# Scores, softmax and weighted values of an attention layer staggered by one step, and the experts' biases summed on another engine

## The chip, the cores and the metric

The kernel runs on one core of one Trainium2 chip. A core has five engines that work side by side and wait for each other by semaphores: TensorE (PE; its weight loads are a row of their own, PEld), VectorE (DVE), ScalarE (ACT), GpSimd (POOL) and SyncE (SP), which here only issues DMAs. The metric is the device time of one execution in microseconds (us).

## The reference, cut to what matters

Two layers work on 8 x 1024 tokens of 256 numbers, in float32. The first is a per-token attention over channels with a layer norm. The second is a transformer block: attention over the 8 positions of the first axis (1024 independent columns, 4 heads of 64), a layer norm, and a mixture of 8 experts with a capacity of 1024 tokens each, then two more layer norms. The parts that the change touches:

```python
qkv = x @ w.T + b
scores = jnp.einsum('nhld,nhmd->nhlm', q, k) / np.float32(np.sqrt(HD))
attn = jax.nn.softmax(scores, axis=-1)
o = jnp.einsum('nhlm,nhmd->nhld', attn, v).transpose(2, 0, 1, 3).reshape(L, N, D)
...
h = jnp.einsum('ecd,edf->ecf', disp, w1) + b1[:, None, :]
y = (jnp.einsum('ecf,efd->ecd', h, w2) + b2[:, None, :]).reshape(E * cap, D)
```

There is no nonlinearity between w1 and w2. So an expert is one matrix w1 w2 (256 x 256) and one bias row b1 w2 + b2, and the kernel works both out once, ahead of the tokens.

## The kernel before, in words

Three phases follow each other. `phase_a` (up to 4336 us) is the first layer. `phase_b` (to 4951 us) is the second layer's attention, its first norm, the router's logits, and, mixed in, the experts' products. `phase_c` routes the tokens, applies the experts and the last norms. The change is in `phase_b` and in a few lines of `phase_c`.

In `phase_b` the order of the instructions on every engine is the order of the program (`manual_schedule`). The loop runs over j from -1 to 8. A group j is 128 columns of the 1024, with 8 positions each: 1024 tokens. Iteration j does the attention of group j, prepares group j + 1 (`nxt`: `turn_x`, `project_qk`, `project_v`), finishes group j - 1 (`prv`: `output`, `normal`, `turn_y`, `logits`) and works out expert j. It has four steps n: a pair of heads c and a half ib of the group's blocks. A step's attention is:

- `scores` (L620): ten products into the tile `sc` (two banks of PSUM), the largest of each row negated by VectorE (L645, L646)
- `weights` (L651), twice: four exponentials each on ScalarE (L654), with their sums
- `normed` (L662): VectorE divides by the sums (L664, L665)
- `turn_s` (L667): eight transposes by TensorE into `pt` (two banks), copied by ScalarE to `sT` (L673)
- `weighted` (L676): sixteen products with the values, copied by ScalarE into `oT` (L691)

Between these the function `some(k)` takes the next k entries from the step's list, which `fills(j)` (L794) writes out by hand. What remains of the list follows at the step's end. All entries and `weighted` use PSUM tiles `fill`, of which there are two. [...] `sc` 2, `pt` 2, `pw` 1, `pb` 1, `fill` 2.

`expert(e, piece)` (L764) adds two of the eight blocks of w1 w2 to `pw` (L773) and, with two products, their part of all biases to `pb` (8 x 256, L781). The left side of those is `b1z`, a block of b1 in one column of eight and zero in the others. `load_expert` (L756) brings a piece's w1 and w2 in at the start of each step, on SP's queue, behind a piece of zeros for `disp_d` (L862, in two of the four steps). In the same queue stand the stores of y (L727). In `phase_c`, sixteen small products (L1000) and four copies (L1007) spread the bias rows `b12` over all partitions; the experts' results get them at L1061.

`output` (L703) begins with `residual`: POOL adds the output bias to x (L698). VectorE then adds the product (L716) and takes statistics (L66, L68), and POOL makes the reciprocal root (L70, L72). `normal` (L719) scales on VectorE (L724), applies gain and bias on POOL (L726) and stores y. `turn_y` (L729) needs that y.

Of the kernel before, what the change touches and what calls it, by code (L numbers as in the profile page):

```python
# [21 lines left out]
FP = mybir.dt.float32  # L22
# [4 lines left out]
ALU = mybir.AluOpType  # L27
# [3 lines left out]
P = 128  # L31
# [13 lines left out]
@with_exitstack  # L45
def fused_kernel(ctx: ExitStack, tc: tile.TileContext, a: dict, out: bass.AP):
    nc = tc.nc

    const = ctx.enter_context(tc.tile_pool(name="const", bufs=1))
    small = ctx.enter_context(tc.tile_pool(name="small", bufs=4))  # L50

    ident = const.tile([P, P], FP, name="ident")
    make_identity(nc, ident)
    mhalf = const.tile([P, 1], FP, name="mhalf")
    nc.gpsimd.memset(mhalf, -0.5)

    dram = ctx.enter_context(tc.tile_pool(name="dram", bufs=1, space=bass.MemoryType.DRAM))
    x1_d = dram.tile([L * N, D], FP, name="x1_d")
    y1_d = dram.tile([L * N, D], FP, name="y1_d")
    disp_d = dram.tile([2 * E * CAP, D], FP, name="disp_d")  # L60
    moe_d = dram.tile([E * CAP + 1, D], FP, name="moe_d")

    def norm_scalars(r):

        st = small.tile([P, 6], FP, name="st")
        nc.vector.bn_stats(out=st, in_=r)  # L66
        mv = small.tile([P, 2], FP, name="mv")
        nc.vector.bn_aggr(out=mv, in_=st)  # L68
        ve = small.tile([P, 1], FP, name="ve")
        nc.gpsimd.tensor_scalar(ve, mv[:, 1:2], EPS, None, ALU.add)  # L70
        rs = small.tile([P, 1], FP, name="rs")
        nc.gpsimd.tensor_tensor(rs, ve, mhalf, ALU.pow)  # L72
        return mv[:, 0:1], rs

    phase_a(tc, a, ident, x1_d, norm_scalars)

    late = ctx.enter_context(tc.tile_pool(name="late", bufs=1))
    w12 = late.tile([P, DC, E, D], FP, name="w12")
    b12 = late.tile([E, D], FP, name="b12")
    lg = late.tile([P, NT, E], FP, name="lg")  # L80
    phase_b(tc, a, ident, x1_d, y1_d, disp_d, w12, b12, lg, norm_scalars)
    phase_c(tc, a, ident, x1_d, y1_d, disp_d, moe_d, w12, b12, lg, norm_scalars, out)


def phase_a(tc, a, ident, x1_d, norm_scalars):
# [417 lines left out]
        store(NT - 1)  # L503


def phase_b(tc, a, ident, x1_d, y1_d, disp_d, w12, b12, lg, norm_scalars):

# [7 lines left out]
    with (  # L515
        tc.tile_pool(name="bw", bufs=1) as wp,
        tc.tile_pool(name="bgroup", bufs=2) as gp,
        tc.tile_pool(name="bx", bufs=3) as xp,
        tc.tile_pool(name="bwork", bufs=2) as kp,
        tc.tile_pool(name="bps", bufs=1, space=PSUM) as p1,  # L520
        tc.tile_pool(name="bfill", bufs=2, space=PSUM) as pf,
        tc.manual_schedule(),
    ):
        wi = wp.tile([P, DC, 3 * D], FP, name="wi")
# [9 lines left out]
        nc.sync.dma_start(wout, a["out_wT"].rearrange("(c p) f -> p c f", p=P))  # L534
        wg = wp.tile([P, DC, E], FP, name="wg")
        nc.sync.dma_start(wg, a["wg"].rearrange("(c p) e -> p c e", p=P))
        nc.sync.dma_start(b12, a["b2"])

        b1r = wp.tile([P, FC, E], FP, name="b1r")
        nc.sync.dma_start(b1r, a["b1T"].rearrange("(c p) e -> p c e", p=P))  # L540
        b1z = wp.tile([P, FC, E, E], FP, name="b1z")
        nc.gpsimd.memset(b1z, 0.0)
        nc.gpsimd.tensor_copy(b1z.rearrange("p c e f -> p c (e f)")[:, :, 0 : E * E : E + 1], b1r)


        rep = wp.tile([P, L, B], BF, name="rep")
# [3 lines left out]
        for h in range(2):  # L550
            r = slice(h * HW, h * HW + B)
            nc.vector.tensor_copy(rep[r], ident[r, None, r].to_broadcast([B, L, B]))
            nc.vector.tensor_scalar(other[r], rep[r], -1.0, MASKED, ALU.add, ALU.mult)
        pb = p1.tile([E, D], FP, name="pb")
        zeros = wp.tile([P, 1024], FP, name="zeros")
        nc.gpsimd.memset(zeros, 0.0)

# [8 lines left out]
        def turn_x(j, l0):  # L566
            if l0 == 0:
                G["xT", j] = wp.tile([P, DC, NB, L, B], FP, name="xT")
                G["qk", j] = gp.tile([P, DC, 2, N], FP, name="qk")
                G["v", j] = gp.tile([P, NB, D], FP, name="v")  # L570
            ps = pf.tile([P, 512], FP, name="fill")
            for l in range(2):
                for c in range(DC):
                    n = 2 * l + c
                    nc.tensor.transpose(
                        ps[:, n * P : (n + 1) * P], G["x", j][:, l0 + l, c * P : (c + 1) * P], ident
                    )
            for l in range(2):
                nc.vector.tensor_copy(
                    G["xT", j][:, :, :, l0 + l, :],  # L580
                    ps[:, l * D : (l + 1) * D].rearrange("p (c b n) -> p c b n", c=DC, n=B),
                )
# [17 lines left out]

        def project_v(j, b0):
            xT = G["xT", j].rearrange("p c b l n -> p c b (l n)")
            ps = pf.tile([P, 512], FP, name="fill")
# [15 lines left out]

        def scores(j, c, ib):  # L620
            qk = G["qk", j]
            sc = p1.tile([P, 2, 512], FP, name="sc")
            prs = [slice(h * HW, (h + 1) * HW) for h in range(2)]
            for h in range(2):
                nc.tensor.matmul(
# [39 lines left out]
            nc.vector.tensor_tensor(s, s, sm[:, :, None].to_broadcast([P, 8, P]), ALU.mult)  # L665

        def turn_s(state):  # L667
            s = state[2]
            pt = p1.tile([P, 2, 512], FP, name="pt")
            for g in range(8):  # L670
                nc.tensor.transpose(pt[:, g // 4, (g % 4) * P : (g % 4 + 1) * P], s[:, g, :], ident)
            sT = kp.tile([P, 8, P], FP, name="sT")
            nc.scalar.copy(sT, pt)  # L673
            return sT
# [89 lines left out]
        def expert(e, piece):  # L764
# [5 lines left out]
            for i in range(2):  # L770
                fc = piece * 2 + i
                for d in range(DC):
# [8 lines left out]
                nc.tensor.matmul(  # L781
                    pb,
                    b1z[:, fc, e, :],
                    w2[:, i, :],
                    start=e == 0 and fc == 0,
                    stop=e == E - 1 and fc == FC - 1,
                    skip_group_check=True,
                )
            if piece == 3:
                nc.scalar.copy(w12[:, :, e, :], pw.rearrange("p (c d) -> p c d", c=DC))  # L790
                if e == E - 1:
                    nc.vector.tensor_tensor(b12, pb, b12, ALU.add)

        def fills(j):  # L794

# [7 lines left out]
            def put(part, ok, fn, *args):  # L803
                if ok:
                    o[part].append((fn, *args))

            put(0, O, output, prv, 0)
            put(0, N, turn_x, nxt, 0)
            put(0, N, turn_x, nxt, 2)
            put(0, O, output, prv, 2)  # L810
            put(0, O, normal, prv, 0)
            put(0, N, turn_x, nxt, 4)
            put(0, N, turn_x, nxt, 6)
            put(0, X, expert, j, 0)
# [27 lines left out]
            put(3, N, project_qk, nxt, 1, 1, 1)  # L842
            return o

        for j in range(-1, NJ + 1):
            if j < 0:
                load_x(0)
# [2 lines left out]
            for n in range(4):  # L850
                work = list(parts[n])

                def some(k):
                    for _ in range(k):
                        if work:
                            fn, *args = work.pop(0)
                            fn(*args)

                if 0 <= j < NJ:
# [7 lines left out]
                    st = scores(j, c, ib)  # L867
                    some(1)
                    weights(st, 0)
                    some(1)  # L870
                    weights(st, 1)
                    normed(st)
                    some(3)
                    sT = turn_s(st)
                    some(1)
                    weighted(j, c, ib, sT)
                some(len(work))
                if n == 2 and 0 <= j and j + 2 < NJ:
                    load_x(j + 2)


def phase_c(tc, a, ident, x1_d, y1_d, disp_d, moe_d, w12, b12, lg, norm_scalars, out):


    nc = tc.nc
# [2 lines left out]
    with (  # L888
# [103 lines left out]
                tc.declare_no_dep(one.ins, other.ins, reason="rows of their own")  # L992
            scattered.append(one)


        bias = op.tile([P, E, D], FP, name="bias")
        for e in range(0, E, 2):
            ps = pp.tile([P, 512], FP, name="ps")
            for i in range(2):
                nc.tensor.matmul(  # L1000
                    ps[:, i * D : (i + 1) * D],
                    ident[0:E, e + i : e + i + 1].to_broadcast([E, P]),
                    b12,
                    start=True,
                    stop=True,
                )
            nc.vector.tensor_copy(bias[:, e : e + 2, :], ps.rearrange("p (e d) -> p e d", e=2))  # L1007
        disp_v = disp_d.rearrange("(e s p) d -> e p s d", p=P, s=SH)
        moe_v = moe_d[0 : E * CAP, :].rearrange("(e s p) d -> e p s d", p=P, s=SH)
        NH = E * ST // SH  # L1010
# [223 lines left out]
```

## Time and profile before

| | us |
|---|---|
| median of 3 runs | 5320.8 (5317.32 to 5326.3) |
| profiled execution, its own time | 5320.41 |
| its span | 5318.7 |
| TensorE busy | 5016.6 (94%) |
| VectorE / ScalarE / POOL busy | 2975.2 / 3361.0 / 3367.1 |
| second phase, first scores to end of the last `weighted` | 4374.8 to 4914.7 |

The span is the time from the first to the last instruction of the profiled execution; 1.7 us of that execution lie around it. "PE fill L683 <- ACT sT L673" means that TensorE stood still before it wrote `fill` at line 683, until ScalarE's write of `sT` at line 673 was done; the numbers after it are the total in us, how often, and the longest. A row of the timeline has the start and the length in us, the engine, line, operation, what is written and read, the shape and how many instructions are merged. A bracket at its end tells the idle time before it and who ended that. A matmul's length holds its way through the pipeline, so the distance between starts tells what a stream of them costs.

### The profile page before, as it was taken

The page shows a single profiled execution, that of the slowest core. Times are in us where ns is not written, and L with a number is a line of the kernel's source. Part 1 is how long each engine was busy: PE and PEld are TensorE (multiplying, and loading weights), DVE is VectorE, ACT ScalarE, POOL GpSimd, SP SyncE. Part 2 cuts the span into 40 slices and gives each one's busy share as a digit, 9 for nine tenths or more (in the row PEclk, how much of TensorE's full clock was granted, in tenths as well). Part 3 has the DMA queues.
Part 4 walks back from the last instruction along what each step waited for, and adds up shares of the span by engine and source line. Part 5 has one row for each costly group of instructions (what it writes and reads, how often), then busy time and mean ns, then how long its engine had stood idle before and what let it go on. Part 6 is the DMA issues. An engine that isn't in the chain of part 4 may idle for free. (4 is left out here: it accounts for less than half of the span.)

```text
span 5318.7 us, 190637 instructions
## 1 busy us (share of the span) xinstructions
PE 5016.6 (94%) x80212; PEld 3384.1 (64%) x80212; DVE 2975.2 (56%) x5849; ACT 3361.0 (63%) x4106; POOL 3367.1 (63%) x6939
## 2 busy tenths in 40 slices
PE   8999999999999999999999999999999978898177
PEld 4666666666666666666666666666666645565166
DVE  5666666666666666666666666666666633433145
ACT  4777777777777777777777777777777743333025
POOL 5776766677777767677676777667676632333625
PEclk9999999999999999999999999999999989999589
DMA  2222222222222222222222222222222221221463
GB/s 74 47 48 48 48 48 48 48 48 48 48 48 48 48 47 48 48 48 48 48 49 47 49 48 48 48 47 49 48 48 48 47 77 65 70 80 56 136 219 98
DMA packets 603424, 313.55 MB, mean 59 GB/s; under 512 B 388154, under 2 KB 562371, under 8 KB 602563
## 3 DMA queue, kind: packets, MB, share of 16 engines
q1 hardware_dynamic: 396130, 147.14, 12.1%
q0 software_dynamic: 202752, 151.40, 9.6%
q8 instruction: 627, 10.27, 0.8%
q10 hardware_dynamic: 3680, 2.83, 0.2%
q14 instruction: 235, 1.92, 0.1%
HBM read 82.76 MB, written 50.33 MB: 25 GB/s over the span
## 5 line engine op out<-in xcount | busy, mean ns | idle before, releaser
L324 ACT ACTIVATE e<-pair 128x1024 f32<-128x1024 f32 x3072 | 2977.4, 1021 | 1237.4 <-PE pair L308 1237.4
L368 POOL DMA_DIRECT2D nd<-S x4096 | 1953.0, 484 | 612.1 <-DVE S L358 420.0
L308 PE MATMUL pair<-R,L 32*128 32x128 f32 (+1 forms) x32768 | 1607.0, 323 | 1.8 <-POOL event L279 1.8
L358 DVE COPY S<-sum 128x512 f32<-128x512 f32 x1024 | 707.1, 691 | 1467.4 <-PE sum L347 1131.6
L308 PEld LDWEIGHTS pair<-R,L 32*128 32x128 f32 x32768 | 1272.4, 186 | 47.9 <-POOL event L279 2.3
L338 PE MATMUL sum<-e,V 128*32 128x256 f32 x16384 | 1285.7, 385 | 4.9 <-DVE S L358 4.9
L265 POOL DMA_DIRECT2D R<-qm x2048 | 973.9, 483 | 73.8 <-issue 38.7
L347 PE MATMUL sum<-e,V 128*32 128x128 f32 x16384 | 823.6, 273 | 0.0
L347 PEld LDWEIGHTS sum<-e,V 128*32 128x32 f32 x16384 | 533.0, 110 | 352.8 <-issue 1.8
L338 PEld LDWEIGHTS sum<-e,V 128*32 128x32 f32 x16384 | 406.5, 109 | 236.8 <-DVE vT L206 41.8
L296 PE MATMUL pair<-late,sel 32*128 32x256 bf16 (+1 forms) x6144 | 499.3, 313 | 9.6 <-ACT e L324 9.6
L219 DVE COPY V<-vT 32x128 f32<-32x128 f32 x2048 | 457.1, 223 | 28.1
L377 DVE RECIPROCAL att<-nd 128x256 f32<-128x256 f32 x256 | 447.4, 1748 | 7.2 <-DMA nd<-S 3.3
L296 PEld LDWEIGHTS <-sel 32*128 32x128 bf16 x6144 | 155.4, 91 | 460.4 <-issue 445.0
L279 POOL MEMSET event<- 1x1 f32 x256 | 22.8, 89 | 615.3 <-DMA R<-qm 403.1
L188 PE MATMUL ps<-wk,xT 128*128 128x512 f32 x512 | 257.8, 626 | 11.7 <-DMA wk<-in_Wk 10.9
L199 PEld LDWEIGHTS ps<-xT,wv 128*128 128x128 f32 x2048 | 238.2, 191 | 44.4 <-issue 41.8
L199 PE MATMUL ps<-xT,wv 128*128 128x128 f32 x2048 | 262.6, 281 | 1.6 <-DVE qm L232 0.8
L70 POOL TENSOR_SCALAR ve<-mv 128x1 f32<-128x1 f32 x128 | 39.4, 308 | 354.6 <-DVE mv L68 353.2
L231 PE MATMUL ps<-wq,xT 128*128 128x512 f32 x512 | 255.7, 622 | 5.8 <-DVE k L189 5.8
L408 PE MATMUL ps<-wo,attT 128*128 128x256 f32 x1024 | 256.7, 394 | 0.7 <-ACT attT L391 0.7
L408 PEld LDWEIGHTS ps<-wo,attT 128*128 128x128 f32 x1024 | 185.3, 191 | 63.3 <-issue 41.8
(171 smaller groups left out, 3962.4 us busy)
## 6 DMA issues: line engine op xcount, KB each, us to landing
R<-qm POOLq DMA_DIRECT2D x2048, 32.0 KB
nd<-S POOLq DMA_DIRECT2D x4096, 16.0 KB
L<-k SPq DMA_DIRECT2D x4088, 8.0 KB
xT<-in_xT SPq DMA_DIRECT2D x64, 128.0 KB
xr<-in_x SPq DMA_DIRECT2D x64, 128.0 KB
x_d<-x1o SPq DMA_DIRECT2D x64, 128.0 KB
x<-x_d SPq DMA_DIRECT2D x8, 1024.0 KB
disp_d<-zeros SPq DMA_DIRECT2D x16, 512.0 KB
```

The source lines that it names most:

```text
L199: nc.tensor.matmul(ps[:, i * P : (i + 1) * P], w["v"][:, c, ch * P : (ch + 1) * P], xT_of[t][:, c, :], start=c == 0, stop=c == DC - 1,)
L219: nc.vector.tensor_copy(V[32 * aa : 32 * aa + 32, qd % 2, :, qd // 2, :, aa, 0:4], src[32 * qd : 32 * qd + 32, :, ww, :, aa, :],)
L265: moved.append((None, nc.gpsimd.dma_start(R[:, b, s, b, :], q[:, b, s, cols])))
L296: nc.tensor.matmul(bank[u].rearrange("p (n i) -> p n i", i=n)[:, :, 0:32], sel[pr].rearrange("p a j -> p (a j)"), late[pr, None, :].to_bro ...
L308: one = nc.tensor.matmul(bank[u][:, x * 4 * n : (x + 1) * 4 * n].rearrange("p (b i) -> p b i", i=n), Lt[pr, 2 * (h0 + h) + jb].rearrange(" ...
L324: nc.scalar.activation(e, pair[i], AF.Exp)
L338: nc.tensor.matmul(dst[32 * u : 32 * u + 32], Vs[ww][:, 0, h0 + h, u, :], e0[u // 2][:, u % 2, x * 256 : (x + 1) * 256].rearrange("p (b i) ...
L347: nc.tensor.matmul(dst[32 * u : 32 * u + 32, :, 32:], Vs[ww][:, 1, h0 + h, u, :], e1[u // 2][:, u % 2, h * 128 : (h + 1) * 128].rearrange( ...
L358: nc.vector.tensor_copy(S[:, :, 2 * which : 2 * which + 2, :].rearrange("p b h i -> p h b i"), ps.rearrange("p (h b i) -> p h b i", h=2, b=4),
L368: nc.gpsimd.dma_start(tok[:, b, s, h0 * C1 : (h0 + G) * C1], Sx[:, 4 if s else b, b, :])
L377: nc.vector.reciprocal(att[:, cols], nd[:, 1, cols])
L408: nc.tensor.matmul(ps[:, :D], attT[:, c, :], wo[:, c, :], start=c == 0, stop=c == HID // P - 1)
```

## The change

A step's weights are no longer turned and used in the same step. The step keeps `(j, c, ib, st)` in `before`, and `turn_s` and `weighted` of it run within the next step: `turn_s` after the first four exponentials of the new scores, `weighted` after `normed`. For the last step of a group that is step 0 of the next iteration, and there `some` holds `output` back until `weighted` is in the program, as `output` reads its result. The transposes go into the score tile of their own step, so `pt` is gone; `sc` has two buffers. With `pb` gone too, `fill` gets a third bank. The list of step 0 is put into another order. `G["v", j]` is taken in `project_v`.

The biases: VectorE adds w2's rows times b1 (one number per partition) to `acc` (128 x 8 x 256), one instruction for each of the 64 blocks. `acc` starts as zeros with b2 in its first partition. One product per expert with a matrix of ones (`expert_bias`) adds up the partitions and puts the row in all of them; ScalarE copies it to `bias`, which `phase_c` now takes as it is.

```diff
-    b12 = late.tile([E, D], FP, name="b12")
+    bias = late.tile([P, E, D], FP, name="bias")
...
+        tc.tile_pool(name="bsc", bufs=2, space=PSUM) as p2,
         tc.tile_pool(name="bps", bufs=1, space=PSUM) as p1,
-        tc.tile_pool(name="bfill", bufs=2, space=PSUM) as pf,
+        tc.tile_pool(name="bfill", bufs=3, space=PSUM) as pf,
...
-        nc.sync.dma_start(b12, a["b2"])
-
-        b1r = wp.tile([P, FC, E], FP, name="b1r")
-        nc.sync.dma_start(b1r, a["b1T"].rearrange("(c p) e -> p c e", p=P))
-        b1z = wp.tile([P, FC, E, E], FP, name="b1z")
-        nc.gpsimd.memset(b1z, 0.0)
-        nc.gpsimd.tensor_copy(b1z.rearrange("p c e f -> p c (e f)")[:, :, 0 : E * E : E + 1], b1r)
+        b1 = wp.tile([P, FC, E], FP, name="b1")
+        nc.sync.dma_start(b1, a["b1T"].rearrange("(c p) e -> p c e", p=P))
+
+        acc = wp.tile([P, E, D], FP, name="acc")
+        nc.gpsimd.memset(acc, 0.0)
+        nc.sync.dma_start(acc[0:1].rearrange("p e d -> p (e d)"), a["b2"].rearrange("(o e) d -> o (e d)", o=1))
+        ones = wp.tile([P, P], FP, name="ones")
+        nc.gpsimd.memset(ones, 1.0)
...
-            sc = p1.tile([P, 2, 512], FP, name="sc")
+            sc = p2.tile([P, 2, 512], FP, name="sc")
...
         def turn_s(state):
-            s = state[2]
-            pt = p1.tile([P, 2, 512], FP, name="pt")
+            pt, s = state[0], state[2]
...
-                nc.tensor.matmul(
-                    pb,
-                    b1z[:, fc, e, :],
-                    w2[:, i, :],
-                    start=e == 0 and fc == 0,
-                    stop=e == E - 1 and fc == FC - 1,
-                    skip_group_check=True,
+                nc.vector.scalar_tensor_tensor(
+                    acc[:, e, :], w2[:, i, :], b1[:, fc, e : e + 1], acc[:, e, :], ALU.mult, ALU.add
                 )
             if piece == 3:
                 nc.scalar.copy(w12[:, :, e, :], pw.rearrange("p (c d) -> p c d", c=DC))
-                if e == E - 1:
-                    nc.vector.tensor_tensor(b12, pb, b12, ALU.add)
+
+        def expert_bias(e):
+            ps = pf.tile([P, 512], FP, name="fill")
+            nc.tensor.matmul(ps[:, :D], ones, acc[:, e, :], start=True, stop=True)
+            nc.scalar.copy(bias[:, e, :], ps[:, :D])
...
-            put(0, O, output, prv, 0)
             put(0, N, turn_x, nxt, 0)
             put(0, N, turn_x, nxt, 2)
+            put(0, N, turn_x, nxt, 4)
+            put(0, not N and O, expert_bias, prv)
+            put(0, not N and X, expert, j, 0)
+            put(0, O, output, prv, 0)
+            put(0, N, turn_x, nxt, 6)
+            put(0, N and O, expert_bias, prv)
             put(0, O, output, prv, 2)
+            put(0, N and X, expert, j, 0)
             put(0, O, normal, prv, 0)
-            put(0, N, turn_x, nxt, 4)
-            put(0, N, turn_x, nxt, 6)
-            put(0, X, expert, j, 0)
             put(0, N, project_qk, nxt, 0, 0, 0)
...
-                        if work:
+
+                        if work and not (n == 0 and before and work[0][0] is output):
...
                     st = scores(j, c, ib)
                     some(1)
                     weights(st, 0)
-                    some(1)
+                if before:
+                    sT = turn_s(before[3])
+                    some(2 if live else 0)
+                if live:
                     weights(st, 1)
                     normed(st)
-                    some(3)
-                    sT = turn_s(st)
-                    some(1)
-                    weighted(j, c, ib, sT)
+                if before:
+                    weighted(*before[:3], sT)
+                before = None
                 some(len(work))
+                if live:
+                    before = j, c, ib, st
...
-        bias = op.tile([P, E, D], FP, name="bias")
-        for e in range(0, E, 2):
-            ps = pp.tile([P, 512], FP, name="ps")
-            for i in range(2):
-                nc.tensor.matmul(
-                    ps[:, i * D : (i + 1) * D],
-                    ident[0:E, e + i : e + i + 1].to_broadcast([E, P]),
-                    b12,
-                    start=True,
-                    stop=True,
-                )
-            nc.vector.tensor_copy(bias[:, e : e + 2, :], ps.rearrange("p (e d) -> p e d", e=2))
```

More of the change, by code (lines that the diff above doesn't have):

```diff
@@ L78, in fused_kernel @@
     w12 = late.tile([P, DC, E, D], FP, name="w12")
-    b12 = late.tile([E, D], FP, name="b12")
+    bias = late.tile([P, E, D], FP, name="bias")
     lg = late.tile([P, NT, E], FP, name="lg")
-    phase_b(tc, a, ident, x1_d, y1_d, disp_d, w12, b12, lg, norm_scalars)
-    phase_c(tc, a, ident, x1_d, y1_d, disp_d, moe_d, w12, b12, lg, norm_scalars, out)
+    phase_b(tc, a, ident, x1_d, y1_d, disp_d, w12, bias, lg, norm_scalars)
+    phase_c(tc, a, ident, x1_d, y1_d, disp_d, moe_d, w12, bias, lg, norm_scalars, out)
 def phase_a(tc, a, ident, x1_d, norm_scalars):
@@ L503, in phase_a, with phase_b @@
         store(NT - 1)
-def phase_b(tc, a, ident, x1_d, y1_d, disp_d, w12, b12, lg, norm_scalars):
+def phase_b(tc, a, ident, x1_d, y1_d, disp_d, w12, bias, lg, norm_scalars):
     nc = tc.nc
@@ L553, in phase_b @@
             nc.vector.tensor_scalar(other[r], rep[r], -1.0, MASKED, ALU.add, ALU.mult)
-        pb = p1.tile([E, D], FP, name="pb")
         zeros = wp.tile([P, 1024], FP, name="zeros")
@@ L569, in turn_x @@
                 G["qk", j] = gp.tile([P, DC, 2, N], FP, name="qk")
-                G["v", j] = gp.tile([P, NB, D], FP, name="v")
             ps = pf.tile([P, 512], FP, name="fill")
@@ L602, in project_v @@
             xT = G["xT", j].rearrange("p c b l n -> p c b (l n)")
+            if b0 == 0:
+                G["v", j] = gp.tile([P, NB, D], FP, name="v")
             ps = pf.tile([P, 512], FP, name="fill")
@@ L854, in some @@
                     for _ in range(k):
-                        if work:
+                        if work and not (n == 0 and before and work[0][0] is output):
                             fn, *args = work.pop(0)
                             fn(*args)
-                if 0 <= j < NJ:
+                live = 0 <= j < NJ
+                if live:
                     if n < 2:
@@ L869, in phase_b, with phase_c @@
                     weights(st, 0)
-                    some(1)
+                if before:
+                    sT = turn_s(before[3])
+                    some(2 if live else 0)
+                if live:
                     weights(st, 1)
                     normed(st)
-                    some(3)
-                    sT = turn_s(st)
-                    some(1)
-                    weighted(j, c, ib, sT)
+                if before:
+                    weighted(*before[:3], sT)
+                before = None
                 some(len(work))
+                if live:
+                    before = j, c, ib, st
                 if n == 2 and 0 <= j and j + 2 < NJ:
                     load_x(j + 2)
-def phase_c(tc, a, ident, x1_d, y1_d, disp_d, moe_d, w12, b12, lg, norm_scalars, out):
+def phase_c(tc, a, ident, x1_d, y1_d, disp_d, moe_d, w12, bias, lg, norm_scalars, out):
     nc = tc.nc
```

## The prediction

> **What bounds the kernel now.** I read the busy shares by stretch first, one stretch per token group of the second phase (j = 1 to 7, then the tail), to see which engine fills the phase.
>
> ```profile
> 4501.06:4572.50 71.44, 63.84 (x377) 42.50 (x376) 27.66 (x60) 26.14 (x85) 23.15 (x28) 0.98 0.23 74
> 4572.50:4642.38 69.88, 62.27 (x377) 41.84 (x377) 27.67 (x60) 26.14 (x85) 23.18 (x28) 1.00 0.24 76
> ...
> 4856.55:4913.64 57.09, 44.38 (x298) 32.49 (x297) 22.71 (x49) 20.87 (x77) 23.27 (x28) 0.88 0.17 56
> 4913.64:4951.00 37.36, 18.39 (x82) 15.32 (x80) 11.57 (x32) 2.93 (x5) 20.10 (x28) 0.71 0.09 29
> ```
>
> Columns: length, then busy PE, weight load, DVE, ACT, POOL, then granted clock. TensorE is busy 62.27 of 69.88 us, every other compute engine under 28, so TensorE's own order bounds a group: its work plus its waits. The 0.98 against 1.00 separates 71.44 from 69.88: a spell of reduced clock costs 71.44 - 69.88 = 1.56 us. Then the waits of TensorE in this phase, to see what it stands still for (total, times, longest):
>
> ```profile
> PE fill L683 <- ACT sT L673: 17.8, 19, 1.2
> PE fill L590 <- ACT yT L739: 7.9, 6, 1.3
> PE fill L708 <- DVE xT L579: 7.7, 6, 1.3
> PE pt L671 <- DVE lg L754: 7.4, 6, 1.2
> PE pt L671 <- DVE s L665: 5.8, 2, 3.2
> PE fill L575 <- DVE xT L579: 5.4, 7, 1.3
> PE fill L747 <- ACT qk L593: 4.7, 6, 0.8
> ```
>
> Two kinds stand here: turned weights that TensorE wants before ScalarE has copied them (L683), and two `fill` banks or one score tile not yet free. With three smaller rows (2.5, 2.0, 1.3) they are 62.5 us over eight groups, 7.61 in the group at 4642 (0.42, 1.28, 0.67, 0.74, 1.32, 0.78, 1.16, 1.24). Last, the timeline of TensorE in that group, for the bias products and for the clock:
>
> ```profile
> 4654.62 1.03 PE L773 MATMUL pw<-w,w 128*128 128x256 f32 x4
> 4655.58 0.60 PE L781 MATMUL pb<-w,b1z 128*8 128x256 f32 x2
> 4656.11 1.13 PE L773 MATMUL pw<-w,w 128*128 128x256 f32 x4
> 4657.17 0.60 PE L781 MATMUL pb<-w,b1z 128*8 128x256 f32 x2
> ...
> 4670.43 1.98 PE L683 MATMUL fill<-sT,v 128*64 128x128 f32 x16 [1.16 <-ACT sT L673]
> ```
>
> An `expert` piece takes 3.08 us (4654.62 to 4657.70). At 4670.43, after waits of 1.32, 0.78 and 1.16, sixteen products take 1.98 instead of 1.09: the spell of reduced clock.
>
> **The change, part by part** (sums against the profiled execution: 5320.41 us, span 5318.7; the median of the runs is 5320.8, 0.4 more).
>
> *Bias products leave TensorE.* Eight 128x256 products with full weights stream in 1.83 us (L708, 4643.59 to 4645.42), so a piece falls from 3.08 to 1.83: 1.25 less, four pieces a group, 5.0. Back comes one 128x256 product per expert, 0.25, with a ScalarE copy of half the 0.59 that 128x512 takes (L691), at a point where ScalarE idles.
>
> *16 products on VectorE per group.* L378 (two SBUF inputs, 128x256) takes 425 ns; 16 x 0.42 = 6.7 us on an engine with 27.7 of 70 busy. Cover: they sit at the end of each step's list, where VectorE idles 3 to 7.7 us before L645. Without it, in step 0, they delay the chain below. From below 0.42 is firm (L232, the same operation at twice the width, 0.69). From above: L665 took 1.91 at 4666.15 instead of 1.22 while POOL's L698 ran from 4665.72 to 4666.98. The Trainium skill, "SBUF — State Buffer", section "Who interferes with whom", says that a DVE instruction with two SBUF inputs and a GpSimd one that reads SBUF exclude each other for the whole instruction. Row and rule differ in price: the row cost 0.69, the rule allows a whole POOL operation, 1.27 (L726), per product, 20 us a group. I take the 0.42 plus 0.3 once in step 0, since POOL is busy a third of the time and two of the four steps have slack; by the rule's worst case step 0 alone loses 2 x 1.27, 18 us over seven groups.
>
> *Turning moves into the next step; two score tiles; three fill banks.* `pt` goes, so `turn_s` finds its weights scaled long before (L671's waits, 13.2, go), and with a third bank L579, L593, L739 and L716 no longer hold one that is wanted (30.2 us). What is late next, per step, from the durations above (us from the step's first product):
> - Step 0: scores to 1.2, `turn_x` 1.7, `turn_s` 2.6, two `turn_x` 3.6. ScalarE's queue now holds: four exponentials (start 2.9, after L645/L646), then sT (4.3 to 5.3), then the other four (to 6.7), then oT (7.3). So `weighted` waits 1.7 (3.7 to 5.4), and `output`, which follows it directly, waits for oT from 6.4 to 7.35: 0.95.
> - Step 0 to 1: L716 of `output` 0 at 9.3 to 10, its statistics to 11.1, POOL's two power pairs to 12.3, xb 13.6; L716 of `output` 2, statistics to 15.5, two new products 16.3 to 16.6, L724 17.2, POOL's two L726 to 19.85. `turn_y` 0, now third in step 1 (which starts at 15.5), is ready at 17.65: a wait of 2.25. In the kernel before it came at once.
> - Behind that store on SP's queue: 512 KB of zeros and the loads for `expert` 1. In the last group w issued until 4903.25 and was used at 4905.90, 2.65 us; with 1.5 for the zeros at the 350 GB/s of the phase's start it lands at about 26, and `expert` 1 comes at 26.5. Cost 0 to 1; I take 0. In the kernel before the same load had 14 us.
> - Steps 2 and 3: `output` 6, `project_qk` and `project_v` cover the 5.3 us to sT; no wait.
>
> New waits 1.7 + 0.95 + 2.25 = 4.9 for the 7.6 removed.
>
> *Clock.* The Trainium skill, "TensorE: Matmul & The Clock Gate", section "Why this matters for your kernels", warns of idle gaps over about 3 us. By that rule neither old nor new waits would matter, and a group keeps its clock (saving 1.6 more each). The trace disagrees: a lone wait of 1.24 was followed by slow products twice, the cluster at 4670 too, and 0.73 + 1.34 in the last group (clock 0.57). The new clusters, 1.7 + 0.95 within 3.7 us and 2.25 in one piece, are longer; I take two spells a group, 3.1, for about one, 1.5.
>
> *Sum.* A usual group: 71.4 = 57.3 work + 5.0 bias + 7.6 waits + 1.5 clock. After: 57.3 + 0.25 + 4.9 + 3.1 = 65.55. Groups 1 to 6 lasted 428.3; 6 x 65.55 = 393.3: -35.0. Group 0 (4374.77 to 4428.31): steps 1 to 3 lose 1.10 wait and 1.25 bias each; step 0 loses `turn_s`, `weighted` and bias but now has six xT copies behind the scaling on VectorE, so L590 starts at 4384.3: -0.3. Together -7.3. Group 7 has no next group to fill it. In the same way its step 0 ends at 10.95 (waits of 1.0 for sT and 0.95 for oT); step 1 at 27.9, as `turn_y` 0 waits 6.3 for POOL's y and `expert` 1 waits 1.1 for its load; steps 2 and 3, waiting for POOL's y and for sT, at 37.2 and 45.5; the last scaling, turning, `weighted` and oT, now with nothing beside them, take 5.1. `output` starts at 50.6 instead of 57.1; less 1.5 for one more spell of clock: -5.0. From there to the logits' end (4913.6 to 4951.0) the chain over POOL stays as it is. Start: acc's memset is twice L556's 0.97 and may hold L70 back by 0.9, and its DMA waits for it on SP before `load_x`; a third bank gives back 0.4: +0.5 (bounds 0 and 2). Third phase: sixteen L1000 and four L1007 run beside the scatters (4969.8 to 5050): 0. If these were not covered they were worth 4 us. Total -47: 5320.4 - 47 = 5273, and 0.4 more against the median: 5274.
>
> **The rivals.**
> - *The new waits are smaller or the clock holds* (for: one group of six kept 1.00 with 7.6 of waits; against: the longest single gap grows from 1.3 to 2.25). Saving per group 5.0 - 0.25 + 7.6 - 3 + 1.5 = 11: 6 x 11 + 7.3 + 6.5 = 79, 5241. Chance 0.12.
> - *The chain over VectorE and POOL into `turn_y` grows*: products meet POOL (2 x 1.27), L724 meets it too (4923.81: 1.34 for 0.41), load late by 1. That is 4 more a group in seven: 47 - 28 = 19, 5301. For: 1.95 for xb at 4648.84. Against: POOL has only 23 busy of 70. Chance 0.13.
> - *Slower: the w1/w2 loads become exposed.* A piece's buffers are now also held by VectorE's products, and the load of step 1 stands behind the y store. Place: L773. Price up to 4.1 a piece (2.65 + 1.5), 32 pieces; it beats the 47 gained from 1.5 us a piece on. At 2.5 it is +80 - 47 = 5354. For: 1.3 us at 4905.90 today. Against: loads at 4674.86 are used at 4689.31. Chance 0.04.
> - *It does not overlap as written* (sT comes after the list in all four steps, as the four exponentials ahead of it on ScalarE would have it where the list is short): the old waits stay, and 1.2 more a step eats the 32 x 1.25 - 2 = 38 of the bias: 5320. Against: only step 0's list is shorter than 5.3 us. Chance 0.03.
>
> **How the numbers follow.** The forecast has 0.68 and its own spread is 5255 to 5292 (zero or three spells, load late or not). The range reaches into both neighbours: 5240 to 5300. About 0.2% (10.6 us) is what a measurement of this kernel can tell from no change. Faster: 0.68 + 0.12 + 0.12 = 0.92; same 0.04; slower 0.04.
>
> **What would show it.** Group length 65 to 66; no L781; L683 waiting for sT once a group, about 1.7; L708 waiting for oT about 0.9; L735 waiting for POOL's y about 2.2; sixteen products at 0.42 on VectorE, some longer; clock about 0.95. Wrong if L773 waits for DMA in most groups, if the groups last over 68, or if the first or third phase moves by more than 3 us.

## The result, and the profile after

The changed kernel takes 5259.73 us (median of 4 runs, 5255.02 to 5262.35), the kernel before 5321.07 (4 runs): a ratio of 0.9883, 95% interval 0.9871 to 0.9895. The forecast was 5274 (5240 to 5300). The profiled execution took 5258.0 us, its span is 5256.2.

First the totals of the engines, from the head of the page: busy time, share of the span, instructions.

```profile
PE 4961.1 (94%) x80084; PEld 3377.1 (64%) x80084; DVE 3013.8 (57%) x5908; ACT 3359.9 (64%) x4114; POOL 3364.5 (64%) x6939
```

TensorE lost 55.5 us of its 5016.6 and is still busy 94% of the span; VectorE gained 38.6: the products that it took over last 43 in all, and some work went, as the four copies at L1007 (2.7). Now the stretches of the second phase, with the columns of before (length, then busy PE, weight load, DVE, ACT, POOL, then granted clock): a usual group, the one of groups 1 to 6 that had a spell of reduced clock (3.41 us at half the clock), group 0, and the first three steps of group 7.

```profile
4425.95:4486.73 60.78, 56.57 (x363) 41.95 (x364) 32.72 (x68) 26.00 (x86) 22.71 (x28) 1.00 0.27 87
4608.87:4671.31 62.44, 58.11 (x363) 43.15 (x363) 33.05 (x68) 26.09 (x86) 22.63 (x28) 0.97 0.26 85
4377.20:4425.95 48.75, 44.45 (x257) 29.94 (x257) 20.01 (x36) 21.78 (x79) 0.00 (x0) 0.93 0.20 66
4792.98:4830.93 37.95, 29.02 (x221) 24.22 (x220) 22.91 (x46) 15.84 (x59) 19.12 (x25) 0.91 0.19 63
```

A usual group fell from 69.88 to 60.78, and its clock is 1.00. What TensorE still waits for in groups 1 to 6 (4425.95 to 4792.98), as total, times and longest:

```profile
PE fill L736 <- POOL y L727: 14.3, 6, 2.4
PE fill L684 <- ACT sT L674: 10.4, 6, 1.7
PE fill L709 <- ACT oT L692: 1.0, 6, 0.2
PE pw L774 <- DMA w<-in_w: 0.3, 1, 0.3
```

In the kernel before, seven rows stood here, 45.2 us in all; now it is 26.0. These are the three waits that the prediction named. Each on TensorE's timeline (start, length, what is written and read; in the bracket the idle time before):

```profile
4614.21 1.09 PE L684 MATMUL fill<-sT,v 128*64 128x128 f32 x16 [1.73 <-ACT sT L674]
4616.10 1.56 PE L709 MATMUL fill<-wout,oT 128*128 128x256 f32 x6 [0.16 <-ACT oT L692]
4567.75 0.66 PE L736 MATMUL fill<-ident,y 128*128 128x128 f32 x4 [2.38 <-POOL y L727]
```

Where the 62.5 us between the two spans came from:

| stretch | before | after | difference | forecast |
|---|---|---|---|---|
| to the first scores | 4374.77 | 4377.20 | +2.4 | +0.5 |
| group 0 | 53.54 | 48.75 | -4.8 | -7.3 |
| groups 1 to 6 | 428.24 | 367.03 | -61.2 | -35.0 |
| group 7, to its first `output` | 57.09 | 57.49 | +0.4 | -5.0 |
| from there to the logits' end | 37.1 | 38.0 | +0.9 | 0 |
| third phase | 367.9 | 367.7 | -0.2 | 0 |

The first row can't be told from what the start varies by: over the fourteen kernels profiled here the first scores came between 4372.2 and 4379.5, with no order that follows what was changed in them.

### The profile page after: what moved, and what is told of

Read it like the earlier page. It is cut to its first block, busy times and chain, and to the rows that moved or that the text cites. A ratio compares the mean times of both kernels' runs of the same rounds, so it can differ in the third digit from the quotient of the medians.

```text
span 5256.2 us, 190381 instructions
## 1 busy us (share of the span) xinstructions
PE 4961.1 (94%) x80084; PEld 3377.1 (64%) x80084; DVE 3013.8 (57%) x5908; ACT 3359.9 (64%) x4114; POOL 3364.5 (64%) x6939
```

## The experiments

Two questions. Which part of the change brought what, and why did the part that was worth most (groups 1 to 6) bring 26 us more than forecast while the ends of the phase brought less? My theory: each of the three parts (bias products, staggered steps, third bank) does what was costed, the chain of POOL's operations into `turn_y` 0 is the largest wait left, and the forecast's clock term was too large. The rival: one part carries it all, and the remaining waits are only where something else shows up. The kernel before ran again beside each set of runs, with medians of 5320.71 to 5322.65; the ratios are to the one beside it, and differences of 2 us between two sets say nothing.

**The change without its third bank.**

```diff
-        tc.tile_pool(name="bfill", bufs=3, space=PSUM) as pf,
+        tc.tile_pool(name="bfill", bufs=2, space=PSUM) as pf,
```

> The changed kernel with two fill banks instead of three. Theory A (the stagger needs the third bank): in step 0 output 2 waits for turn_x 6's copies, which stand behind the statistics on VectorE, about 1.9 us, and project_qk in step 1 for output 4's bank, about 1; some 3 us a group, 5280 (5273 to 5288). Theory B (the stagger and the two score tiles alone remove the waits): within 4 us of the changed kernel, 5256 to 5264.

5273.07 us (5267.34 to 5277.46), ratio to before 0.9903 (0.9887 to 0.992): 13.3 above the changed kernel, at the low end of theory A. A usual group lasts 63.40. Some of its waits in groups 1 to 6:

```profile
PE fill L590 <- DVE r L717: 7.4, 6, 1.2
PE fill L736 <- POOL y L727: 6.6, 6, 1.1
PE fill L684 <- ACT yT L740: 3.9, 6, 0.7
PE fill L709 <- ACT bias L791: 2.8, 6, 0.5
```

Rows 1, 3 and 4 wait for a reader of a bank, and the third bank removes them. But L736 waits 1.1 here and 2.4 with three banks: TensorE comes earlier to a y that is ready no sooner. All waits come to 35.5 against 26.0: 9.5 less in six groups, or 1.6 a group, of the 2.57 that the group got shorter.

**The biases alone**, in the kernel before: VectorE's products and one product per expert in place of `pb`, nothing staggered, two `fill` banks.

```diff
-                nc.tensor.matmul(pb, b1z[:, fc, e, :], w2[:, i, :], ...)
+                nc.vector.scalar_tensor_tensor(
+                    acc[:, e, :], w2[:, i, :], b1[:, fc, e : e + 1], acc[:, e, :], ALU.mult, ALU.add
+                )
```

> The kernel before with only the biases summed on VectorE and by one product an expert; order, pt and two fill banks as before. Theory A (TensorE bounds the phase and the products lie beside it): 32 pieces x 1.25 less 8 x 0.25 = 38 less, 5283. Rival (the waits that the bias products filled come back, as the turned weights are no earlier): only the pieces that do not stand between turn_s and weighted or before turn_s gain, about half, 5302. Slower than 5315 would mean that VectorE's products hold up the copies that free the banks.

5298.62 us (5293.0 to 5304.44), ratio 0.9951 (0.9935 to 0.9968): 24 faster than before instead of 38. Its only undisturbed group, and a usual one:

```profile
4567.87:4633.03 65.16, 57.65 (x364) 41.85 (x365) 33.27 (x68) 26.46 (x86) 23.53 (x28) 1.00 0.25 81
4633.03:4701.49 68.46, 60.94 (x364) 44.47 (x364) 33.24 (x68) 26.47 (x86) 23.50 (x28) 0.95 0.24 77
```

65.16 against 69.88 is -4.72, as costed (5.0 less 0.25). The time is near the rival's, but not for its reason: the waits did not come back (7.29 in this group, 7.61 before). In groups 1 to 6 the rest went to the clock, with eleven spells where the kernel before had six.

**The biases and a third bank**, still not staggered: the same, with `bufs=3` for `fill`.

> The kernel before with the biases on VectorE and the bank so freed given to fill (three), order as before. Theory A (the stagger is needed for the turned weights, the bank takes only its own waits): of 30 us of bank waits about half go, the waits for sT and for the scaling (31 us) stay or grow: 5268 (5260 to 5277), slower than the changed kernel by 8. Rival (banks are all that mattered, the stagger brought nothing): 5253 or less, as fast as the changed kernel or faster.

5296.2 us (5293.87 to 5296.6), ratio 0.995 (0.9934 to 0.9967). Both forecasts missed: without the stagger a third bank is worth 2 us, which is within the spread of the runs. Some of its waits in the whole second phase:

```profile
PE pt L671 <- DVE s L665: 27.4, 15, 4.1
PE fill L683 <- ACT sT L673: 20.5, 19, 1.1
...
PE pt L671 <- DVE lg L754: 8.2, 7, 1.2
```

In groups 1 to 6 the waits for a bank are gone, and TensorE now arrives at `turn_s` before VectorE has scaled the weights, 15 times. Here the bank saves little, as what comes next in the order is not ready.

**The stagger alone**: the changed kernel with `pb` back on TensorE, and so two `fill` banks.

```diff
-                nc.vector.scalar_tensor_tensor(acc[:, e, :], ...)
+                nc.tensor.matmul(pb, b1z[:, fc, e, :], w2[:, i, :], ...)
```

> The changed kernel with the bias products back on TensorE (pb takes the third fill bank, so two) and the bias rows spread in the third phase as before. Theory A (bias products cost 1.25 a piece at any place): slower than the two-bank run above by 38, about 5318, so that stagger without the bias part would gain next to nothing. Rival (the bias products fill waits that the stagger leaves): slower by under 25, 5305 or less.

5307.37 us (5304.57 to 5313.09), ratio 0.9972 (0.996 to 0.9983): 15 faster than before, and 34 slower than the kernel with both and two banks, between the two forecasts. A quiet group is 4.01 longer than with two banks and the biases on VectorE (67.41 against 63.40): 5.1 more work, and 1.1 less of waits, which the products cover. So the four versions give -15 for the stagger, -24 for the biases, -49.6 for both, and -13 more for the bank once both are there (-2 without the stagger). Stagger and biases together bring 10 more than the sum of the two. The spells fit that: in groups 1 to 6 of the profiled executions the kernel before had six, the biases alone eleven, the stagger alone two, and both with two banks two. Whether that is all of it is not shown, as the waits differ too.

**A longer chain on POOL.** `normal` 0 gets one more POOL operation, a sum with zeros, ahead of the store of y.

```diff
+            if l0 == 0:
+                nc.gpsimd.tensor_tensor(y, y, zeros[:, 0:512].rearrange("p (l d) -> p l d", l=2), ALU.add)
```

> The changed kernel with one more POOL operation (adds a tile of zeros, 1.27 us) before the store of y in the first part of a group, so that TensorE's wait before turn_y 0 grows from 2.4 to about 3.7. Theory A, of the prediction (a longer wait brings a spell of reduced clock): 7 groups x 1.27 plus some 6 spells x 1.5, +18: 5278, and a clock under 0.98 in groups 1 to 6. Theory B (a single wait of this length does not change the clock; the spells of the kernel before came from several waits close together with logits between them): +9, 5269, clock 1.00 in most groups.

5279.89 us (5278.62 to 5283.78), ratio 0.992 (0.9904 to 0.9937), 20 above the changed kernel: theory A. The wait before `turn_y` 0 grew from 2.38 to 3.7, by about the length of the new operation (1.27), and every one of the six groups got a spell:

```profile
4428.09:4491.86 63.77, 58.23 (x363) 43.24 (x363) 32.90 (x68) 26.05 (x86) 23.79 (x29) 0.97 0.25 83
```

So POOL's chain is exposed one to one, and 3.7 is long enough for the clock where 2.38 mostly is not.

**`turn_y` 0 later in step 1.** The list of step 1 has `project_qk`, `output` 4 and a `project_v` ahead of what needs y.

```diff
-            put(1, O, turn_y, prv, 0)
-            put(1, O, output, prv, 4)
             put(1, N, project_qk, nxt, 0, 0, 1)
-            put(1, O, logits, prv, 0)
+            put(1, O, output, prv, 4)
+            put(1, O, turn_y, prv, 0)
             put(1, O, normal, prv, 4)
+            put(1, N, project_v, nxt, 0)
+            put(1, O, logits, prv, 0)
...
-            put(1, N, project_v, nxt, 0)
```

> The changed kernel with step 1's list reordered: project_qk and output 4 before turn_y 0, project_v before logits 0. Theory A (the wait for POOL's y is pure loss and can be covered by work that is ready): -2.4 in six groups, group 7 unchanged or 2 less: 5244. Rival (the wait moves: the exponentials of the second half now stand behind project_qk's copy on ScalarE and weighted waits for sT, or output 4 reaches VectorE later and y 2 and y 4 with it): 5254 or more.

5259.53 us (5253.89 to 5269.98), ratio 0.9879 (0.9863 to 0.9896): no gain, the rival's number. The wait at L736 is gone from groups 1 to 6, and another has its place:

```profile
PE fill L608 <- DVE r L717: 12.5, 6, 2.1
```

`project_v` needs the bank of `output` 4. That is read by VectorE's r, which needs xb of `output` 4, and xb stands on POOL behind both y of the group. The chain was not left, only entered at another point. Four of six groups had a spell.

**The first `expert` piece ahead of `weighted`** in step 0, to cover the wait for sT.

```diff
-            put(0, not N and X, expert, j, 0)
+            put(0, X, expert, j, 0)
...
-                    some(2 if live else 0)
+                    some((3 if n == 0 else 2) if live else 0)
```

> The changed kernel with expert piece 0 put ahead of weighted in step 0 (as group 7 has it already), into the wait of 1.73 for sT. Theory A (step 0 gets shorter but the chain through VectorE and POOL to y starts at the same time, so the wait before turn_y 0 grows by what is saved): 5260, no change. Rival (the wait at sT is pure loss): -1.7 in six groups, 5250.

5269.18 us (5265.02 to 5270.52), ratio 0.9898 (0.9882 to 0.9915): 9.5 slower than the changed kernel. Slower was in neither forecast. Step 0 fell from 15.01 to 13.46, as meant, but `output` 0, 2 and so POOL's chain start no earlier, and the wait before `turn_y` 0 became 3.56. Again each of the six groups had a spell:

```profile
4425.35:4487.44 62.09, 58.37 (x364) 42.93 (x364) 33.51 (x68) 25.95 (x86) 22.58 (x28) 0.97 0.26 85
```

**Both reorderings.**

> Both reorderings together. If each is right by theory A, the wait before turn_y 0 no longer takes back what step 0 saves: -2.4 and -1.7 in six groups, 5235. If the chain to y bounds steps 0 and 1 whatever stands between, the time is that of the first reordering alone, 5244.

5259.27 us (5257.47 to 5265.6), ratio 0.9886 (0.987 to 0.9903). A quiet group was down to 60.26, with 2.1 before L608 again and 1.2 for sT (L684) in step 1, and three of six groups had a spell. Neither number came. None of three reorderings of TensorE's work had gained anything, so the chain on POOL itself was next.

**POOL's xb early.** The four sums of x and the output bias leave `output` and are issued together as step 0 begins, into four buffers of their own. POOL is idle there.

```diff
+            if j >= 1:
+                for l0 in range(0, L, 2):
+                    residual(j - 1, l0)
...
-            xb = residual(j, l0)
+            xb = G["xb", j, l0]
```

> The changed kernel with POOL's four sums of x and the output bias (xb) of a group issued at the begin of the next group's step 0, into four buffers of their own, instead of each within its `output`. Theory A: POOL stands on the chain from `output` 0 to the first `turn_y` with xb of `output` 2 (1.75 us) between its power pairs and its y; without it the wait before `turn_y` 0 falls from 2.4 to about 0.6, six groups lose 10.5, group 7 and the end of the logits 3 to 6: about 5245 (5240 to 5250). Rival: the wait only moves (five us of POOL sums in a row collide with VectorE's instructions of two SBUF inputs in step 0, and the statistics or the scaling come later): 5256 or more.

5239.97 us (5237.55 to 5241.99), ratio 0.9845 (0.9829 to 0.9862): 19.8 faster than the changed kernel, theory A at its low end. The wait before `turn_y` 0:

```profile
4499.56 0.66 PE L737 MATMUL fill<-ident,y 128*128 128x128 f32 x4 [0.67 <-POOL y L728]
```

It was to be 0.6 and is 0.67. The table of stretches gives -9.5 for groups 1 to 6, -2.4 for group 7 and -2.6 for the rest of the logits.

**All three.**

> The two reorderings together (the first `expert` piece before `weighted` in step 0; `turn_y` 0 behind the next entries in step 1) and POOL's early sums as well. Theory A: both waits of the changed kernel are covered by the order, and the 2.1 that `project_v` waited for VectorE's r, which waits for xb, goes with the early sums: a quiet group falls from 60.26 to about 58.2, with fewer spells of reduced clock: about 5238. Rival: the early sums collide with VectorE as in the kernel with them alone, or the spells stay: no better than the two reorderings, 5259.

5224.74 us (5216.31 to 5232.45), ratio 0.9822 (0.9806 to 0.9838): 13 below theory A's number. In the profiled execution, its quickest, a usual group lasts 56.64, of which 56.48 is busy, and none of the six had a spell. Apart from 0.2 for oT, one wait is left in two of the six groups, the one that the prediction's third rival was about:

```profile
4503.30 1.97 PE L775 MATMUL pw<-w,w 128*128 128x256 f32 x8 [0.98 <-DMA w<-in_w]
```

The same reorderings that were worth nothing with xb late are worth 15 us with it early.

**A wait filled with unused products**, to see what makes the clock fall. The kernel with the first `expert` piece early gets ten products ahead of `turn_y` 0, and step 1 takes one entry more there, so that the rest keeps its place.

```diff
+        def busy():
+            ps = pf.tile([P, 512], FP, name="fill")
+            for i in range(10):
+                nc.tensor.matmul(ps[:, :D], ones, acc[:, 0, :], start=True, stop=True)
...
+            put(1, O and N, busy)
```

> The kernel with the first `expert` piece ahead of `weighted` (a wait of 3.56 before `turn_y` 0, a spell of reduced clock in all of six groups, 5269) with ten products of 128x256 whose result is not used, put into that wait in groups 1 to 6. Theory A (the spell comes from TensorE standing still): no spell in step 1, 6 x 1.3 less, about 5261, and a clock of 1.00 in these groups. Theory B (the spell has another cause, or the products only push later work back): 5269 or more.

5259.6 us (5254.83 to 5260.14), ratio 0.9883 (0.9866 to 0.9899): theory A, 9.6 faster than without the products. Group 1, and the products in group 2 (twenty records, since one float32 product has two):

```profile
4423.01:4483.99 60.98, 60.82 (x383) 45.56 (x382) 33.52 (x68) 26.05 (x86) 22.71 (x28) 1.00 0.27 87
4499.59 4.48 PE L796 MATMUL fill<-acc,ones 128*128 128x256 f32 x20
4503.91 0.60 PE L736 MATMUL fill<-ident,y 128*128 128x128 f32 x4
```

They took 4.3 us, more than the 3.56 of the wait, and all six groups are still shorter (60.98 against 62.09) because no spell follows. So here it is TensorE's standing still that costs the clock.

**The best version**: the three together, w1 and w2 of every piece loaded one step ahead, all of group 0's `turn_x` ahead of the scaling, and acc's zeros behind the first loads of x.

```diff
+            put(0, not O, turn_x, nxt, 6)
...
-                    load_expert(j, n)
+                    if n < 3 or j + 1 < NJ:
+                        load_expert(*divmod(4 * j + n + 1, 4))
```

> All three of the last reorderings, and three more: acc's memset and its load of b2 behind the load of the first x; every piece's w1 and w2 loaded one step ahead, and so ahead of the y stores in SP's queue; in group 0 all of `turn_x` ahead of the scaling. Theory A: the start loses 2, group 0 3 to 6 (L590 no longer waits 3.47 for xT), group 7 its wait of 1.5 for the load and some of the late exponentials: about 5230. Rival: group 7 is held by the chain over POOL, and the start and group 0 by spells of reduced clock, so it stays at the time of the three reorderings without these.

5210.34 us (5206.89 to 5211.52), ratio to before 0.9789 (0.9772 to 0.9805): 49 faster than the changed kernel, 20 below theory A's number. Group 0, a group after it, and all that TensorE waits for in groups 1 to 6:

```profile
4373.96:4416.16 42.20, 41.38 (x258) 28.65 (x258) 20.11 (x36) 21.78 (x79) 0.00 (x0) 1.00 0.26 88
4416.16:4472.80 56.64, 56.48 (x365) 41.72 (x365) 33.92 (x68) 25.67 (x86) 22.52 (x28) 1.00 0.30 94
```

```profile
PE fill L706 <- ACT oT L689: 1.0, 6, 0.2
```

These groups are TensorE's own work now. Against the changed kernel's profile: group 0 -6.5 (the order of `turn_x`), groups 1 to 6 -27.2, group 7 -6.6, the logits after it -5.1. The start shows nothing that its own spread does not cover. In group 7 and after it, 16.4 of waits for POOL's y are left.

## Why the prediction was right or wrong, point by point

The total fell into the range, 14 below the forecast. In the profiled execution groups 1 to 6 gave 26.2 more than forecast and all else gave 10.5 less. That the two partly cancel is luck.

*What bounds a group* was right. That its length is TensorE's busy time and waits is true by definition; what shows the bound is that an undisturbed group got shorter by just what left TensorE (-4.72) while VectorE was busy for 33.27 instead of 27.67, and that with nearly no waits left (the best version) a group lasts TensorE's 56.48 and 0.16.

*Bias products* were right: -4.72 a group for them alone, where 5.0 less 0.25 was worked out.

*Products on VectorE*: 16 a group were counted, and there are 8. The bias products that they replace had been counted by TensorE's records, of which a float32 product has two. At 0.42 and 0.3 once, the true number would have been 3.7 us a group; it is 5.8. In each of groups 1 to 6 the pairs of steps 0 and 3 take 0.97 to 1.00, those of steps 1 and 2 take 1.89. There the first product takes 0.48, and the second, beside POOL's L727, 1.37. The shortest, median and longest of the 64 products, in ns, then two of the pairs, with the POOL operation beside the slow one:

```profile
L782 DVE SCALAR_TENSOR_TENSOR acc<-w,b,acc x64: 452/484/1377, 4386.4 to 4839.2; 128x256 f32<-128x256 f32 x64
4501.90 0.97 DVE L782 SCALAR_TENSOR_TENSOR acc<-w,b,acc 128x256 f32<-128x256 f32 x2
4514.99 1.89 DVE L782 SCALAR_TENSOR_TENSOR acc<-w,b,acc 128x256 f32<-128x256 f32 x2
4515.21 1.38 POOL L727 TENSOR_TENSOR y<-y,row_ln_g 128x512 f32<-128x512 f32 x1 [0.58 <-issue]
...
4831.80 1.88 DVE L782 SCALAR_TENSOR_TENSOR acc<-w,b,acc 128x256 f32<-128x256 f32 x2
4834.85 1.21 DVE L648 TENSOR_SCALAR mx<-mx 128x8 f32<-128x8 f32 x1
```

So the price was the rule's and not the row's: the second product lasts as long as POOL's operation, as the Trainium skill ("SBUF — State Buffer", "Who interferes with whom") has it, where two SBUF inputs contend with POOL's reads and the shared port pair is an exclusive lock. It struck 14 of the 64. But only step 0's pair stands in the chain to `turn_y` 0, and it cost 0.97 where 1.14 was put. TensorE waited for none of the others in these groups, so having taken the row's price cost nothing. The last two rows are from group 7: there a late pair comes ahead of the next scores' maximum, and the tiny L648, 0.17 to 0.25 in groups 1 to 6, took 1.21 beside POOL's L699. No kernel here has that pair at another place, so how much of group 7's loss it makes is not shown.

*Waits that the stagger makes*: sT 1.73 (1.7 worked out), POOL's y 2.38 (2.25), oT 0.16 instead of 0.95. The last was a slip: oT is ready at the time worked out (7.17 us from the step's start, against 7.3), but the first product of `output`, two records at L709, goes ahead of it without a wait. Only the rest reads the new oT.

*A group's work* was put at 57.55 and is 56.55 busy. The work of before had been read as its busy time, and that shrinks when waits go: the changed kernel with two banks runs the same 363 or 364 records in 57.46 busy with nine waits a group, 56.55 with three. So a wait costs the stream somewhat more than the idle time in its bracket, here 0.15.

*Clock*: this is the step that failed. Two spells a group (3.1 us) were assumed because the new waits, 1.7 with 0.95 and 2.25 alone, are longer than the old. One spell came in six groups, 0.3 a group. The 0.95 was not there, and a wait of 1.73 or 2.38 alone costs the clock only if it falls into the wrong place (last section). With 0.6 from the waits and 1.0 from the work, this 2.8 makes up the difference between 65.55 and the 61.17 that a group took, and six times that is the 26 us.

So groups 1 to 6 went the way of the first rival, to whom a group was worth 11 us (it was 10.2); the total stayed between that rival's 5241 and the forecast because the ends gave less:

*Group 0* gained 4.8 instead of 7.3. The prediction put `turn_x` behind the scaling on VectorE, which was right, but took the wait for its own length only:

```profile
4386.60 3.75 PE L590 MATMUL fill<-xT,wi 128*128 128x512 f32 x4 [3.47 <-DVE xT L579]
```

A wait of 3.47, and the four records after it take 3.75 instead of 1.99: a spell. In the best version, with the copies ahead of the scaling, group 0 has a clock of 1.00 and is 6.5 shorter.

*Group 7* gained nothing instead of 5.0. Steps 0 to 2 took 10.42, 17.95 and 9.58, to 37.95 where 37.2 was worked out. Step 3 and the last `turn_s` were misjudged:

```profile
4838.80 2.85 PE L774 MATMUL pw<-w,w 128*128 128x256 f32 x8 [1.50 <-DMA w<-in_w]
4845.33 1.07 PE L672 MATMUL sc<-ident,s 128*128 128x128 f32 x8 [1.91 <-DVE s L667]
```

The loads for the last piece stand on SP's queue behind a y store (issued 4834.83, the loads at 4835.30 and 4835.76), where the prediction put nothing for the last piece; and the last scaling ended 52.2 us after the group's start, not 46.9 (45.5 and the 1.4 of a scaling). The loads one step ahead, in the best version, remove the L774 row.

*Start*: +0.5 is within what the start varies by; nothing can be said of it. *Third phase*: 0 was right.

## What to carry to other kernels

Before moving work on the bounding engine, follow the chain that it waits for and shorten that first: three reorderings gained nothing while POOL's sums stood inside the chain, and 15 us once they were out. A further buffer is worth what the next wait in the order allows (about nothing or 13 us for the same bank). Price each wait with what the clock does after it, and look at the first and last turn of the loop on their own: they lack the neighbours that hide things in the middle.

## What the runs showed of the hardware

The clock goes by more than the longest wait: it goes by where a wait falls. In each of the fourteen traces, all spells of the second phase begin on one even grid with steps of 3.41 us and last whole steps (in groups 1 to 6 one or two), at a clock of 0.50. Half of 3.41 is 1.7; groups with one short spell are 1.4 to 1.7 longer. Groups 4 and 5 of the changed kernel have the same waits. These are steps of its grid around the wait of 2.38 before `turn_y` 0, with the columns of before:

```profile
4624.69:4628.10 3.41, 1.50 (x18) 1.14 (x14) 3.38 (x7) 0.91 (x5) 2.90 (x4) 1.00 0.00 0
4628.10:4631.51 3.41, 2.94 (x9) 2.58 (x10) 0.57 (x1) 3.30 (x14) 3.05 (x4) 0.50 0.65 217
...
4686.13:4689.54 3.41, 2.50 (x27) 1.92 (x26) 3.31 (x9) 0.69 (x1) 2.85 (x5) 1.00 0.00 0
4689.54:4692.95 3.41, 1.93 (x11) 1.78 (x12) 1.57 (x2) 3.31 (x13) 3.01 (x3) 1.00 0.34 123
4692.95:4696.37 3.42, 3.42 (x26) 1.96 (x24) 1.17 (x3) 1.58 (x7) 2.14 (x2) 1.00 1.02 335
```

In group 4 most of the wait falls into one step, TensorE is busy for only 1.50 of it, and the next step has a clock of 0.50. In group 5 the grid cuts the wait in two, and the clock stays at 1.00. In groups 1 to 6 of the fourteen traces 58 steps at full clock were followed by a spell. Counting the logits' products of eight columns as standing still, TensorE stood still for at least 1.69 us in all 58, about half a step, and in only 19 of the 1418 others. This was counted in traces taken for other ends: no run moved a wait along the grid or changed the logits alone.

So a lone wait of 3.56 to 3.7 brought a spell in 12 of 12 groups (two kernels): it fills half a step wherever it falls. Waits of 2.0 to 2.4 did in 8 of 18 (three kernels), 1.73 in 3 of 24 (four kernels). The kernel before and the one with the biases alone have no wait over 1.32 in these groups and 17 spells: 7 after the lone 1.24 behind logits, 6 at the cluster of 1.32, 0.78 and 1.16 with logits in it, 4 at 0.42 and 1.28. The Trainium skill's "No PE-idle gaps" over about 3 us ("TensorE: Matmul & The Clock Gate", "Why this matters for your kernels") is therefore no safe bound here. The free-running window of 3.4 us that its section "What's actually happening" gives agrees with the grid; by the count above, the idle window that it names need be idle only for about half.

The grid may also be why the biases alone had so many spells: most of their groups last 68.2 to 68.5, and twenty steps are 68.3, so the same waits meet the grid in nearly the same place each time. That is not shown.
